# Moving the left-hand block loads of a graph kernel's layer products by one place in the load queue

## The chip, the cores and the metric

The kernel runs on one core of one Trainium2 chip. The metric is the time of the program on the device in microseconds (us), the median of several runs. A profiled execution has a time of its own, and the trace covers its span.

## The reference, cut to what matters

Two graph layers over 3327 nodes (padded to 26 tiles of 128) with 512 features, all in float32:

```python
h = relu(layernorm(x))
q, k, v = h @ Wq.T + bq, h @ Wk.T + bk, h @ Wv.T + bv
x = x + softmax(q @ k.T / sqrt(512) + 2 * adj) @ v      # layer 0
h = relu(layernorm(x))
A2 = adj + eye;  d = diagonal(A2) ** -0.5
x = x + relu((d[:, None] * A2 * d) @ (A2 @ h @ W.T))    # layer 1
```

What costs time are the scores q @ k.T and three large products of a 3328 x 3328 matrix with a 3328 x 512 one: softmax weights times h (g = 0 below), A2 times h (g = 1), A2 times the scaled rows (g = 2).

## The kernel before, in words

**Stages.** First h, its transposes and the projection of the queries; then 52 steps of scores (four groups of 13), which store the weights, with their block sums, in DRAM tensors p; then the layer products. Every product is cut after Strassen's scheme into seven products of half blocks, and each of these once more into seven, so that blocks are added and subtracted by VectorE and multiplied by TensorE.

**The layer products** are 294 steps, built as `Step` (L701): three products g, seven outer products r in the order p5, p1, p6, p7, p2, p3, p4, two strips s of the output, and seven values of t (0 to 5 and None). So number k = ((g * 7 + r) * 2 + s) * 7 + t. A step needs

- a left-hand block `a`, loaded by `Step.load` (L708) through `left` (L680): two DMAs of 448 KB (strip 0) or 384 KB (strip 1), one if t is None. They read p (L688), the sums (L691) or adjT (L695). The blocks lie in a ring of five views (`a_ring`, L673), so that the block of step m takes the view of step m - 5.
- sums of its quarters, by `Step.sums` (L711, three VectorE instructions at L164 to L166), traced two steps ahead.
- a right-hand block, loaded by `Right.load` (L622, DMAs at L620 and L634) five steps ahead and combined by `Right.make` three steps ahead. The loads whose place would be in front of step 0 are in the list `early` (L1213).

`Step.multiply` gives 14 matmul instructions (L732), or 8 where t is None (L723).

**What sets the order.** `run(k)` (L1313) traces one step, and the block `in_order` (L112, L1379) chains the instructions of VectorE, TensorE, GpSimd, ScalarE and SyncE each in the order in which they are traced. Nearly all loads are issued by SyncE (SP); its queue thus follows the text of `run`. Iteration k traces in this order: the left-hand block of step k + 3; the functions that `between[k]` holds and whose names have the word load; the matmuls of step k; `deliver(k)` (L933), which issues stores that were put off; sums of step k + 2; and the remaining functions of `between[k]`. An SP instruction that waits holds up all behind it.

**Other work that SP gets between the steps**: `prepare` (L879, iteration 2: four DMAs of weights, one of a bias, and the diagonal of adjT, `dg`, element by element), `load_diagonal` (L886, iteration 5: the diagonal once more, four DMAs into `by_32`), `Job.load` (iterations 7 to about 161), `other_weights` (L906, iteration 154: four DMAs), `Columns.reload` and `Columns.load` (in g = 2), and the stores of `Columns.add` (L1197), four DMAs in rows of 128 bytes for each of 14 pieces of the output. These are put off by `later` steps and issued by `deliver`. Other stores (`post`, L930) go through ScalarE's queue. `judge` (L834, iteration 8) checks the row sums of the softmax: six small VectorE instructions and then a matmul at L848, which TensorE meets between steps 8 and 9.

The blocks of steps 0 to 2 are loaded during the scores (`openers`), the later ones in `run`:

```python
        if k + 3 < len(steps):
            steps[k + 3].load()
```

Of the kernel before, what the change touches and what calls it, by code (L numbers as in the profile page):

```python
# [47 lines left out]
def graph_layers_kernel(  # L48
# [49 lines left out]
    def bank(k, name):  # L98
        return banks.tile([P, BW], F32, name=name, tag=f"bank{k}")
# [647 lines left out]
    steps = [(n, t) for n in range(len(groups)) for t in range(HALF)]  # L747
# [36 lines left out]
    with in_order(*(e.engine for e in (nc.vector, nc.tensor, nc.gpsimd, nc.sync))):  # L784
# [11 lines left out]
        k = len(steps)  # L796
# [32 lines left out]
    def banks_for(*names):  # L829
        return {r: bank(ROLE[r], r) for r in names}  # L830
# [102 lines left out]
    def deliver(before):  # L933
        while posted and posted[0][0] < before:
            posted.pop(0)[1]()

    def set_up():

        free = [view(k, j)[:, 2 * m : 2 * m + 2] for k, j in ((2, 2), (3, 0), (3, 1), (3, 2)) for m in range(2)]
        free = [f.rearrange("p a w -> p (a w)") for f in free] + [mid(k, [P, H[0]], f"ct{k}") for k in range(10)]  # L940
        for s in range(2):
            cts[s] = [[free.pop()[:, : H[s]] for d in range(DC)] for y in range(2)]
        cts["to"] = [free.pop() for k in range(2)]
# [202 lines left out]
    def turn_last(i):  # L1146
        turned_last[i] = turned(i, LAST[i - 20])
# [54 lines left out]
    steps = [Step(g, r, s, t, rights[g, r, t]) for g in range(3) for r in ORDER for s in range(2) for t in every]  # L1202
# [4 lines left out]
    def number_of(g, r, s, t):  # L1207
        return ((g * len(ORDER) + r) * 2 + s) * len(every) + t

    def at(k, what, *args):  # L1210
        between.setdefault(k, []).append((what, args))

    early = []  # L1213
    for g in range(3):
        for n, r in enumerate(ORDER):
            for t, e in enumerate(every):
                k = number_of(g, n, 0, t)
# [11 lines left out]
    for n, job in enumerate(jobs):  # L1229
        k = k0 + n * (k1 - k0) // len(jobs)  # L1230
# [10 lines left out]
    k = number_of(0, 5, 1, 2)  # L1241
# [6 lines left out]
    k = number_of(1, 5, 1, 2)  # L1248
# [8 lines left out]
    k = number_of(2, 4, 0, 0)  # L1257
# [14 lines left out]
    k = number_of(1, 4, 0, 0)  # L1272
# [2 lines left out]
        at(k + 3 + n, difference)  # L1275
    at(k + 8, turn_sign)

    for what in early:
        for _ in what() or ():
            pass  # L1280
# [4 lines left out]
    def flow(tasks):  # L1285
        for what, args in tasks:
            yield from what(*args) or (None,)

    def first_of(parts):
        while parts:  # L1290
            for _ in parts[0]:
                yield
            parts.pop(0)

    def do(part, n=None):
        for _ in itertools.islice(part, n):
            pass
# [3 lines left out]
    def begin(k, j):  # L1301
        if (k, j) not in begun:
            begun.add((k, j))
            for w, n in inserted.get((k, j), ()):
                w.product(n)

    def coming(k):
        r, s = steps[k].r, steps[k].s
        gathers[r, s] = Gather(r, s, k == len(steps) - len(every))
        coming_banks.update(banks_for("p2", "p3", "p4"))  # L1310
        gathers[r, s].seed(coming_banks, ("p2", "p3", "p4"))

    def run(k):  # L1313
        step, now[0] = steps[k], k
        if k == 0:
            set_up()
            coming(0)
        if k + 3 < len(steps):
            steps[k + 3].load()
        if step.t == 0:  # L1320
            banks_of.update(banks_for("p6", "p7", "p5"), **coming_banks, **banks_for("p1"))
        t = step.t
        for what, args in between.get(k, ()):
            if "load" in what.__name__:
                what(*args)
        gatherer = gathers[step.r, step.s]
        weighs = any((k, j) in inserted for j in range(7))
        if k in sums_of and not waiting:
            do(sums_of.pop(k)())
        for j, _ in enumerate(itertools.chain((None,), step.multiply(banks_of))):  # L1330
            begin(k, j)
            if j == 4 and t == PAIRS - 1 and gatherer.last:
                gatherer.first(banks_of)
            if j == (1 if k and steps[k - 1].t is None else 2) and k in sums_of:

                sums = sums_of.pop(k)()
                do(sums, 4)
                waiting.insert(1, sums)
            elif weighs and j > 0:
                do(first_of(waiting), 2)  # L1340
        deliver(k)
        if t is None:
            if not gatherer.last:
                gatherer.rest(banks_of, ("p2", "p3", "p4"))
                begin(k + 1, 0)
                coming(k + 1)
            do(first_of(waiting))
            if gatherer.last:
                flags.append(nc.values_load(bad, min_val=0, max_val=1))
                for n, names in enumerate((("p2", "p3"), ("p4", "p8"))):  # L1350
                    gatherer.rest(banks_of, names)
                    for i in range(20 + 3 * n, 23 + 3 * n):
                        turn_last(i)
            else:
                gatherer.rest(banks_of, ("p8",))
        added = 2 + (t is None)
        waiting.append(steps[k + 2].sums() if k + 2 < len(steps) else iter(()))
        if t == PAIRS - 1 and not gatherer.last:
            do(first_of(waiting))
            gatherer.first(banks_of)  # L1360
        if t == PAIRS - 1:
            banks_of["p8"] = bank(ROLE["p1"], "p8")
            gatherer.seed(banks_of, ("p8",))
        if t is None and gatherer.r == "p7":
            settle = gatherer.settle()
            resting.extend((itertools.islice(settle, 2), settle))
            added -= 1
        elif t is None:
            waiting.append(gatherer.settle())
        elif resting:  # L1370
            waiting.append(resting.pop(0))
            added += 1
        waiting.append(flow([(what, args) for what, args in between.get(k, ()) if "load" not in what.__name__]))
        if (k + 1, 0) not in inserted and (k + 1, 1) not in inserted:
            do(first_of(waiting))
        while len(waiting) > added:
            do(waiting.pop(0))

    with in_order(*(e.engine for e in (nc.vector, nc.tensor, nc.gpsimd, nc.scalar, nc.sync))):  # L1379
        for k in range(len(steps)):  # L1380
            run(k)
        deliver(len(steps))
        now[0] = len(steps)
        for i in range(20, NT, 2):
            finish(i, nc.scalar)
        deliver(len(steps) + 1)
# [378 lines left out]
```

## Time and profile before

| what | value |
|---|---|
| median of 3 runs | 2150.86 us (2150.09 to 2152.09) |
| the profiled execution | 2151.03 us |
| its span in the trace | 2149.1 us |
| TensorE clock granted | 0.999 of full speed |
| TensorE (PE) matmuls busy | 2136.7 us, 99% |
| VectorE (DVE) busy | 1653.3 us, 77% |
| ScalarE (ACT) busy | 274.0 us, 13% |
| DMA | 592.10 MB, 276 GB/s in the mean |
| SP's queue (q1) | 374056 packets, 532.72 MB |
| left-hand blocks (`part`) | 546 DMAs on SP, 3.8 to 6.0 us from issue to landing (medians by kind) |
| step of 14 matmuls | 5.26 us in strip 0, 4.52 us in strip 1 |

In lines of the profile, PE is a matmul, PEld a weight load, SPq an instruction of SyncE's queue. L164 is line 164 of the kernel. `part<-p` is an instruction that writes a tile of the name part from one named p; `<-DVE most L845` behind a time says what ended the idle time before. The chain of work that ended last is followed back from the end, at each step to what released it.

### The profile page before, as it was taken

What the parts mean: (1) busy time and instruction counts of PE and PEld (TensorE: products, weight loads), DVE (VectorE), ACT (ScalarE), POOL (GpSimd) and SP (SyncE); (2) the same over time, 40 slices, a digit from 0 to 9 for tenths busy, and PEclk for the clock granted to TensorE, in tenths of its full rate; (3) what the DMA queues carried; (4) which work ended last, traced back from release to release, by engine and by line L of the source; (5) the groups of instructions that cost most, each with busy time, mean ns of one, the idle gap of its engine ahead of it and who ended that gap; (6) DMA issues with size and microseconds to landing.
All of it is one profiled execution on the core that took longest, in us unless ns stands there. A gap on an engine that the chain in (4) does not pass through costs nothing.

```text
span 2149.1 us, 20906 instructions
## 1 busy us (share of the span) xinstructions
PE 2136.7 (99%) x6272; PEld 1181.0 (55%) x6272; DVE 1653.3 (77%) x3235; ACT 274.0 (13%) x441; POOL 67.5 (3%) x63
## 2 busy tenths in 40 slices
PE   9999999999999999999999999999999999999998
PEld 5555555555555555555454555555666665555554
DVE  7479888888897688776777778787466666788888
ACT  5312221112110000001111000000111100000000
POOL 2000000000003000000111000000000000000000
PEclk9999999999999999999999999999999999999999
DMA  8678888888999899888787889986656578978897
GB/s 301 216 255 294 298 308 286 307 291 287 345 309 299 292 369 335 284 301 303 263 306 266 301 281 360 326 313 225 194 158 210 155 210 255 303 224 249 267 284 190
DMA packets 402498, 592.10 MB, mean 276 GB/s; under 512 B 139964, under 2 KB 273480, under 8 KB 402376
## 3 DMA queue, kind: packets, MB, share of 16 engines
q1 hardware_dynamic: 374056, 532.72, 75.2%
q10 hardware_dynamic: 28320, 57.95, 7.3%
q8 instruction: 52, 0.85, 0.2%
q14 instruction: 70, 0.57, 0.1%
HBM read 422.71 MB, written 173.87 MB: 278 GB/s over the span
## 4 chain that ended last, share of the span: by engine, by line
PE 94%; DVE 3%; DMA 1%; issue 1%; POOL 0%; SPq 0%; ACT 0%; DVEq 0%
PE p L732 55%; PE Y L542 13%; PE Z L542 6%; PE p L723 5%; PE p L1056 4%; PE pw L1117 4%; PE X L542 3%; PE Y L398 2%; PE Z L398 1%; PE X L398 0%; DMA wk<-in_wk_dram 0%; DVE part L164 0%; DVE st L185 0%; DMA part<-sum 0%; DMA part<-p 0%
## 5 line engine op out<-in xcount | busy, mean ns | idle before, releaser
L732 PE MATMUL p<-part,b 128*128 128x448 f32 (+1 forms) x3528 | 1257.7, 513 | 0.4 <-ACT p L986 0.2
L732 PEld LDWEIGHTS p<-part,b 128*128 128x128 f32 x3528 | 669.7, 190 | 542.0 <-issue 291.7
L164 DVE TENSOR_TENSOR part<-part 128x896 f32<-128x896 f32 (+1 forms) x252 | 256.7, 1019 | 67.5 <-DMA part<-p 24.2
L542 PE MATMUL Y<-qt,hp 128*128 128x448 f32 (+1 forms) x832 | 308.1, 513 | 0.1
L542 PEld LDWEIGHTS Y<-qt,hp 128*128 128x128 f32 x832 | 157.9, 190 | 133.0 <-issue 73.0
L542 PE MATMUL Z<-qt,hp 128*128 128x384 f32 (+1 forms) x416 | 162.2, 512 | 0.0
L166 DVE TENSOR_TENSOR part<-part,part 128x448 f32<-128x448 f32 (+1 forms) x219 | 129.5, 591 | 15.0
L165 DVE TENSOR_TENSOR part<-part,part 128x448 f32<-128x448 f32 (+1 forms) x219 | 129.4, 591 | 7.3
L723 PE MATMUL p<-part,b 128*128 128x448 f32 (+1 forms) x336 | 124.2, 512 | 0.0
L542 PEld LDWEIGHTS Z<-qt,hp 128*128 128x128 f32 x416 | 79.0, 190 | 66.2 <-issue 37.9
L546 DVE SCALAR_TENSOR_TENSOR g<-g,Y 128x384 f32<-128x384 f32 (+1 forms) x156 | 91.5, 586 | 30.0 <-PE Y L542 28.8
L992 ACT COPY part<-p 128x384 f32<-128x384 f32 (+1 forms) x33 | 16.6, 503 | 656.4 <-PE p L732 466.6
L723 PEld LDWEIGHTS p<-part,b 128*128 128x128 f32 x336 | 63.8, 190 | 54.1 <-issue 31.2
L549 ACT ACTIVATE g<-g 128x768 f32<-128x768 f32 (+1 forms) x48 | 43.1, 898 | 345.7 <-DVE g L546 288.0
L542 PE MATMUL X<-qt,hp 128*128 128x384 f32 (+1 forms) x208 | 81.1, 512 | 0.0
L993 DVE TENSOR_TENSOR part<-p,part 128x384 f32<-128x384 f32 (+1 forms) x33 | 19.3, 585 | 66.0 <-PE p L732 58.4
L1056 PE MATMUL p<-w,ct 128*128 128x512 f32 x136 | 61.6, 592 | 0.0
L542 PEld LDWEIGHTS X<-qt,hp 128*128 128x128 f32 x208 | 39.5, 190 | 33.1 <-issue 19.3
L191 POOL TENSOR_TENSOR rstd<-ve,mhalf 128x1 f32<-128x1 f32 x46 | 38.4, 836 | 528.5 <-DVE ve L189 500.6
L1012 DVE TENSOR_TENSOR ct<-p,part 128x448 f32<-128x448 f32 (+1 forms) x72 | 42.3, 609 | 15.9 <-PE p L723 11.8
L1117 PE MATMUL pw<-w,rows 128*128 128x256 f32 x208 | 53.4, 379 | 0.0
L1047 DVE TENSOR_TENSOR job<-job 128x896 f32<-128x896 f32 (+1 forms) x52 | 52.9, 1018 | 0.0
(194 smaller groups left out, 1680.7 us busy)
## 6 DMA issues: line engine op xcount, KB each, us to landing
part<-sum SPq DMA_DIRECT2D x104, 448.0 KB, 5.0
part<-p SPq DMA_DIRECT2D x91, 448.0 KB, 6.0
part<-sum SPq DMA_DIRECT2D x104, 384.0 KB, 4.2
part<-p SPq DMA_DIRECT2D x91, 384.0 KB, 4.8
part<-in_adjT_dram SPq DMA_DIRECT2D x78, 448.0 KB, 5.0
b<-row SPq DMA_DIRECT2D x234, 128.0 KB, 4.8
part<-in_adjT_dram SPq DMA_DIRECT2D x78, 384.0 KB, 3.8
g<-in_adjT_dram SPq DMA_DIRECT2D x52, 448.0 KB, 4.1
```

What stands on the lines that cost most here:

```text
L164: yield nc.vector.tensor_add(o[:, 0:2], g[:, 0:4:3], g[:, 1:2].to_broadcast([P, 2, g.shape[-1]]))
L165: yield nc.vector.tensor_add(o[:, 2], o[:, 1], g[:, 0])
L166: yield nc.vector.tensor_add(o[:, 3], o[:, 2], g[:, 2])
L398: nc.tensor.matmul(ps[:, :w], M[B[name]][:, c, o * P : (o + 1) * P], hp[k][:, A[name], c], start=start and c == 0, stop=c == 1, skip_group ...
L542: nc.tensor.matmul(ps[:, :wd], h_of(self.t, name, k), qt[B[name]][:, k], start=start and k == 0, stop=k == 1, skip_group_check=True)
L546: nc.vector.scalar_tensor_tensor(a[n], a[n], 2.0, ps[:, :wd], op0=ALU.mult, op1=ALU.add if sign > 0 else ALU.subtract)
L549: nc.scalar.activation(g[1], g[1], AF.Exp, **({"bias": pad} if self.t == HALF - 1 else {}))
L723: yield nc.tensor.matmul(ps[("p2", "p3", "p4", "p8")[k]][:, :w], b[:, z], a[:, 0, y], start=k == 3 and not self.seeded, stop=True, skip_gr ...
L732: yield nc.tensor.matmul(ps[r][:, :w], b[:, i], m, start=self.t == 0 and not adds, stop=self.t == PAIRS - 1 and r in ("p1", "p5", "p6", "p ...
L1047: nc.vector.tensor_add(self.a, self.a, self.b)
L1056: nc.tensor.matmul(ps, cts[s][y][d][:, k * P : (k + 1) * P], w[d], start=d == 0, stop=d == DC - 1)
L1117: nc.tensor.matmul(ps, a, W[B[name]][:, c], start=new and c == 0, stop=c == 1, skip_group_check=True)
```

## The change

The block of step 3 is loaded ahead of the list `early`; in `run` the load of a left-hand block comes behind the other loads of the iteration and is that of step k + 4. The ring keeps its five views.

```diff
+    steps[3].load()
     for what in early:
         for _ in what() or ():
             pass
...
         if k == 0:
             set_up()
             coming(0)
-        if k + 3 < len(steps):
-            steps[k + 3].load()
         if step.t == 0:
             banks_of.update(banks_for("p6", "p7", "p5"), **coming_banks, **banks_for("p1"))
         t = step.t
         for what, args in between.get(k, ()):
             if "load" in what.__name__:
                 what(*args)
+        if k + 4 < len(steps):
+            steps[k + 4].load()
         gatherer = gathers[step.r, step.s]
```

## The prediction

> **What bounds the kernel now.** I read the page first: the busy shares and the chain that ended last.
>
> ```profile
> PE 2136.7 (99%) x6272; PEld 1181.0 (55%) x6272; DVE 1653.3 (77%) x3235; ACT 274.0 (13%) x441; POOL 67.5 (3%) x63
> PE 94%; DVE 3%; DMA 1%; issue 1%; POOL 0%; SPq 0%; ACT 0%; DVEq 0%
> ```
>
> TensorE is busy for 2136.7 of 2149.1 us, which leaves 12.4 us. Next I asked where these lie, with the busy time by stretch (columns: the stretch, its length, then busy us and instruction count of PE, PEld, DVE, ACT, POOL, then clock, DMA share, GB/s).
>
> ```profile
> 640.00:660.00 20.00, 19.84 (x57) 10.31 (x56) 11.84 (x23) 1.23 (x5) 1.73 (x1) 1.00 0.91 180
> 660.00:680.00 20.00, 19.41 (x64) 11.23 (x63) 13.27 (x33) 0.63 (x2) 9.00 (x2) 1.00 1.00 374
> 1700.00:2140.00 440.00, 440.00 (x1294) 245.39 (x1293) 342.20 (x624) 28.41 (x57) 0.00 (x0) 1.00 0.83 248
> sum 1540.00, PE 1538.52 PEld 852.77 DVE 1164.99 ACT 126.54 POOL 48.40; mean PE 153.85 PEld 85.28 DVE 116.50 ACT 12.65 POOL 4.84
> ```
>
> The sum runs from 600 to 2140 us, which holds the end of the scores and all layer products: PE idles 1540.00 - 1538.52 = 1.48 us in it. The rest lies in the start and in the last stores, which the change doesn't touch. The largest piece of the 1.48 is in 660 to 680. The PE timeline and the chain there say what it is:
>
> ```profile
> 664.85 0.21 PE L848 MATMUL p<-good,ones 128*1 128x26 f32 x2 [0.59 <-DVE most L845]
> ```
>
> ```profile
> 655.61 6.00 DMA part<-p
> 661.73 0.97 DVE part L164
> 664.70 0.10 DVE most L845
> ```
>
> The matmul of judge (L848), which PE meets between steps 8 and 9, waits 0.59 us for VectorE. VectorE does judge's work behind the sums of step 10, in the order of the program, and these waited for step 10's left-hand block, issued at 655.61 and landed at 661.61. So a late load costs PE time here although step 10 itself is far off. Why it was issued so late, SP's timeline tells:
>
> ```profile
> 627.72 1.00 SPq L688 DMA_DIRECT2D part<-p  x2
> 628.77 2.01 SPq L870 DMA_DIRECT2D w<-in_wvT_dram  x4
> 630.82 1.05 SPq L882 DMA_DIRECT2D bv_sb<-in_bv_dram  x1
> 631.92 0.67 SPq L884 DMA_DIRECT2D dg<-in_adjT_dram  x1
> 632.69 8.71 SPq L688 DMA_DIRECT2D part<-p  x5
> 641.70 10.89 SPq L889 DMA_DIRECT2D by<-in_adjT_dram  x4
> 652.70 3.28 SPq L688 DMA_DIRECT2D part<-p  x4
> ```
>
> By the ring of five, and counting issues, the rows are: the two DMAs of step 5's block; prepare's six; the blocks of steps 6 (one DMA), 7 and 8 (two each); the four of load_diagonal; the blocks of steps 9 and 10. The 8.71 us hold one issue of 6.53 us, step 6's, straight behind dg; a free one takes 0.38.
>
> [...] only 13 KB each, yet the issue behind dg takes 6.53 us and the second of load_diagonal's 6.22, against 0.38 for a 448 KB block. [...] So what stands ahead in SP's queue counts, also for a transfer without a wait. [...] SP's waits for PE are its largest:
>
> ```profile
> SPq L691 <- PE p L732: 224.3, 106, 8.7
> SPq L1197 <- DMA xr<-x1d: 10.3, 1, 10.3
> ```
>
> [...] 84 matmuls take 31.57 us (0.376 each) or 27.09 us (0.3225), stage after stage.
>
> **The change part by part.** Call L(m) the block load of step m, O(i) the other loads of iteration i, D(i) the stores that deliver puts on SP in it, F(i) what else it issues on SP. SP's order is the program's. Before: L(i+3) O(i) D(i) F(i) | L(i+4) O(i+1). After: O(i) L(i+4) D(i) F(i) | O(i+1) L(i+5). Nothing stands between O(i) and L(i+4) but D(i) and F(i), so **where these are empty the queue is the same, instruction for instruction**. Nor does a slot come free sooner: five views, L(m) waits for step m-5 as before. "Four in front" is the place in the text, not the time. No DMA, wait or buffer is added or taken away, and PE, VectorE and ACT get the same work in the same order. What moves, from the code:
>
> (1) L(3), two DMAs, goes ahead of the early right-hand loads (four DMAs of rows). By the count of issues, step 3's block goes out at 594.01 and 604.77 us; its first use is at 622.93 (VectorE's sums). Both sets are issued between 576 and 616, beside full PE. A step earlier or later: 0.
>
> (2) L(6), one DMA, goes ahead of prepare (F(2): four, one and one DMAs, 2.01 + 1.05 + 0.67 us). L(6)'s view was step 1's; the first half of that view is read by PE only in step 1's first two matmuls. PE began step 0's last eight at 622.10, so step 1 at 622.10 + 8 x 0.376 = 625.1; the view is free by some 626, SP arrives at 628.77: no wait. Prepare moves back by one issue, 0.4 to 0.5 us. Then the long issue behind dg falls on L(7). dg lands at 640.29; one block more lies ahead of it, 448 KB at some 378 GB/s (the DMA view's rate at that time) = 1.2 us. The long issue ended 1.07 us ahead of dg's landing (632.69 + 6.53 = 639.22), so now by 640.4; three issues at 0.47 follow: 641.85. load_diagonal began at 641.70, released by the matmul of the totals (L818), with SP free since 641.40. So it starts at about 641.9: **+0.2 us**, and with it L(9), L(10), the sums of step 10, judge, and PE. Bounds: 0 if the long issue keeps its length (632.59 + 0.47 + 0.10 + 6.53 = 639.7, ready by 641.1, hidden by L818's release), and +0.9 if the block's whole 1.2 us comes on top of SP's 641.40.
>
> (3) L(158), two DMAs, goes ahead of other_weights (F(154): four DMAs of 256 KB). They are first needed three iterations on; PE shows no stall from 1360 to 1660. 0.
>
> (4) In the last layer L(261), L(264) and so on to L(291) go ahead of the eleven D of four 128-byte-row stores each. A set costs SP 3.5 to 5.4 us of issue (one 12.49, with the 10.3 us wait above), and lies now behind a block instead of ahead of it. The block comes up to that much earlier; the stores, and the O(i+1) behind them, up to one step (4.5 us) later. Gain for PE: it loses nothing from 1700 to 2140, so 0. Cost: a block is issued near the end of step m-5, four steps of 4.515 us (27.09 / 6) = 18.1 before its use; less 6 us landing and 2.1 for its sums (0.96 + 0.56 + 0.56), **10 us of slack**. The right-hand loads have five steps. A turned buffer comes back after nine steps. 0. If the cover were gone, each us past 10 is a us.
>
> The sum: +0.2, on the profiled execution's 2151.03 (span 2149.1 and 1.93 around it): 2151.2. The median of the runs shown is 0.17 lower: 2151.0.
>
> **The rivals.** *Slower, by the boundary*: load_diagonal starts later than hidden, because prepare is pushed by more than one issue, or dg drains later. From 641.70 on each us of SP is a us of PE, through L(10), VectorE's order and judge. For it: the 0.59 us stall, no slack on this chain. Against: SP has 0.3 us in hand and L(6) needn't wait. Were the whole of step 1 awaited (630.4), prepare would move by 1.7 + 0.5, and the price would be 2.2 - 0.3 = 1.9 us: 2152.8.
>
> *Slower, by a block behind a long wait*: L1197 waits 10.3 us for ACT's load of xr, with which it shares no data[...]. With another order such a wait can fall where a whole row of blocks queues behind it. It decides from 10 us of lateness; say 15, so 5 us: 2156. Against: in the one case seen, blocks behind the 12.49 us set didn't stop PE.
>
> *Faster*: blocks ahead of slow stores and of prepare end VectorE's waits and PE's small gaps. The page bounds it: 1.48 us in all, of which 0.59 at judge: 2149.9. Against: the gaps aren't at the stores.
>
> *It doesn't do what it says* is my forecast's own core: the queue keeps its order.
>
> **How the numbers follow.** Forecast, own range 2150.2 to 2152.0: 0.60. Slower by the boundary, to 2153.2: 0.17. Faster, down to 2149.4: 0.16. Behind a long wait: 0.07. The range 2149.4 to 2153.2 leaves out the last and some tails of the others (runs of one kernel differ by 2 us here). About 0.2% (4.3 us) is what a measurement of this kernel can tell from no change. More than 1.48 us can't be won from the part that changes, so faster gets only 0.02, out of its case's 0.16, for what I can't see; slower 0.08, the long wait's 0.07 and 0.01 of the boundary's; within 0.2%: 0.90.
>
> **What would show it.** In SP's timeline three block issues in a row near 627.7, prepare after them, a long issue on step 7's block, load_diagonal at 641.7 to 641.9; PE's wait at L848 0.5 to 0.9 us; in the last layer the same stores each behind one more pair of blocks; PE idle from 600 to 2140 between 1.2 and 2 us. Wrong would be: new PE waits for VectorE or ACT anywhere in the layers, load_diagonal past 643, or a clearly different order on PE.

## The result, and the profile after

| | before | after |
|---|---|---|
| median | 2150.86 us (2148.88 to 2152.65, 7 runs) | 2158.15 us (2155.94 to 2159.91, 7 runs) |
| profiled execution | 2151.03 us, span 2149.1 | 2159.91 us, span 2157.8 |
| TensorE clock granted | 0.999 | 0.997 |

The ratio of after to before is 1.0034, 95% interval 1.0025 to 1.0044: 7.3 us slower, and outside the predicted range. What happened, as the experiments below show, is the rival to which the prediction gave 0.07, a block behind a long wait.

The page of the kernel after, busy shares and the chain that ended last:

```profile
PE 2140.6 (99%) x6272; PEld 1182.7 (55%) x6272; DVE 1653.8 (77%) x3235; ACT 273.2 (13%) x441; POOL 68.5 (3%) x63
PE 93%; DVE 3%; DMA 2%; issue 1%; ACT 0%; POOL 0%; SPq 0%; ACTq 0%; DVEq 0%
```

Here one sees almost nothing: the shares are those of before, except that 1% of the chain has gone from PE to DMA. The busy time by stretch, with the columns as in the prediction, has it:

```profile
640.00:660.00 20.00, 19.82 (x57) 10.30 (x56) 12.19 (x24) 1.22 (x5) 1.56 (x1) 1.00 0.92 186
660.00:680.00 20.00, 20.00 (x66) 11.62 (x65) 13.09 (x33) 0.70 (x2) 11.62 (x2) 1.00 0.98 354
1700.00:2140.00 440.00, 435.16 (x1272) 242.42 (x1271) 337.22 (x616) 28.01 (x56) 0.00 (x0) 0.99 0.82 246
```

PE now stands still for 440.00 - 435.16 = 4.84 us in the last product, where it lost nothing before. The small hole at 660 to 680 is gone. PE's timeline says that the 4.84 us are one wait, ahead of step 287 (the first of strip 1 of the last outer product):

```profile
2108.91 3.17 PE L723 MATMUL p<-part,b 128*128 128x448 f32 x8
2116.92 13.34 PE L732 MATMUL p<-part,b 128*128 128x384 f32 x34 [4.84 <-DVE part L993]
```

The eight matmuls (L723) are step 286. L993 is VectorE's work on the results of step 285, and the work from there on frees the banks (the pieces of memory that hold the results of matmuls) which step 287 writes. So PE doesn't wait for its own block at all; it waits for an instruction that stands behind that block's sums in VectorE's order. VectorE's timeline of the same kernel:

```profile
2114.11 0.96 DVE L164 TENSOR_TENSOR part<-part 128x768 f32<-128x768 f32 x1 [8.41 <-DMA part<-in_adjT_dram]
2116.24 0.62 DVE L993 TENSOR_TENSOR part<-p,part 128x448 f32<-128x448 f32 x1
```

VectorE stood 8.41 us for the left-hand block of step 287. In the kernel before the same two began at 2104.26 and 2106.39, without a wait. SP's timeline of the kernel after, from where the block should have gone out:

```profile
2088.44 6.94 SPq L1197 DMA_DIRECT2D out_dram<-turned  x4
2096.39 0.36 SPq L695 DMA_DIRECT2D part<-in_adjT_dram  x1
2107.55 0.34 SPq L1181 DMA_DIRECT2D part<-x1c  x1
2107.99 3.63 SPq L695 DMA_DIRECT2D part<-in_adjT_dram  x4
2111.68 4.53 SPq L1197 DMA_DIRECT2D out_dram<-turned  x4
```

and of the kernel before, at the same place:

```profile
2094.11 0.33 SPq L1181 DMA_DIRECT2D part<-x1c  x1
2094.53 1.36 SPq L695 DMA_DIRECT2D part<-in_adjT_dram  x2
2095.94 12.49 SPq L1197 DMA_DIRECT2D out_dram<-turned  x4
2108.53 2.83 SPq L695 DMA_DIRECT2D part<-in_adjT_dram  x4
```

Before, the block of step 287 (the two DMAs at 2094.53) went out and then SP stood still inside a set of stores. After, SP stands still from 2096.75 to 2107.55, ahead of a right-hand load (L1181), and the blocks of steps 287 and 288 are behind it. SP's waits in the kernel after say for what:

```profile
SPq L1181 <- DMA xr<-x1d: 10.7, 1, 10.7
SPq L695 <- DMA xr<-x1d: 2.0, 2, 1.8
```

It is the wait of before, now at other instructions: for the load of `xr`, which ACT issues (`last_load`, L1135) and which has no data in common with a block. ACT can't issue it sooner, because the six `xr` loads stand behind a copy (L992) that waits for a matmul ending at 2104.57; the first goes out at 2105.32 (before: 2104.70).

The whole way is in the chain that ended last (start, length, what):

```profile
2104.60 0.54 ACT part L992
...
2106.30 2.25 DMA xr<-x1d
...
2108.62 5.42 DMA part<-in_adjT_dram
...
2114.11 0.97 DVE part L164
...
2116.24 0.63 DVE part L993
...
2116.92 29.47 PE p L732 x84
```

The way leads from PE to ACT, to ACT's load, over a semaphore (a counter on which an instruction waits; SP went on at 2108.57, 0.02 us after the `xr` load had landed) to SP's block load, to VectorE and back to PE. The last row holds a second loss: the same 84 matmuls took 27.09 us before, 2.38 less. The stretches behind the wait show why (the last three columns are clock, DMA share, GB/s):

```profile
2112.00:2117.00 5.00, 0.16 (x2) 0.09 (x1) 2.65 (x5) 0.00 (x0) 0.00 (x0) 0.74 1.09 312
2117.00:2122.00 5.00, 5.00 (x9) 2.82 (x10) 4.97 (x10) 0.00 (x0) 0.00 (x0) 0.58 1.00 310
2122.00:2127.00 5.00, 5.00 (x17) 2.98 (x16) 4.86 (x8) 0.00 (x0) 0.00 (x0) 1.00 1.11 337
```

The clock fell while PE stood still. Means of 0.74 and 0.58 are those of a clock of 0.5 from 2114.4 to 2121.2, 6.8 us (stretches of 2 us give 0.50 from 2116 to 2120), and PE got through 9 matmuls in 5 us instead of 17. It fell 2.3 us after PE had stopped (2108.91 + 3.17 = 2112.08) and rose 4.3 us after PE had set in again at 2116.92.

From the start of step 286's matmuls to that of the last such group is 2146.22 - 2108.91 = 37.31 us, and was 2138.39 - 2108.28 = 30.11: 7.20 us = 4.84 + 2.38 within rounding. Of the profiled executions' difference the rest is 0.63 us before step 286, the balance of small waits (the largest, 0.84 us near 1318, isn't in every run of the new order: `after_fill5` lacks it), and 0.9 in the end.

### The profile page after: what moved, and what is told of

The parts are those of the page before. It is cut to its first block, busy times and chain, and to the rows that moved or that the text cites. A ratio compares the mean times of both kernels' runs of the same rounds, so it can differ in the third digit from the quotient of the medians.

```text
span 2157.8 us, 20907 instructions
## 1 busy us (share of the span) xinstructions
PE 2140.6 (99%) x6272; PEld 1182.7 (55%) x6272; DVE 1653.8 (77%) x3235; ACT 273.2 (13%) x441; POOL 68.5 (3%) x63
## 4 chain that ended last, share of the span: by engine, by line
PE 93%; DVE 3%; DMA 2%; issue 1%; ACT 0%; POOL 0%; SPq 0%; ACTq 0%; DVEq 0%
PE p L732 54%; PE Y L542 13%; PE Z L542 6%; PE p L723 5%; PE p L1056 4%; PE pw L1117 4%; PE X L542 3%; PE Y L398 2%; PE Z L398 1%; DMA part<-sum 1%; DVE part L164 1%; DMA xt<-in_x_dram 1%; PE X L398 1%; DVE part L165 0%; DMA sum<-job 0%
## 5 line engine op out<-in xcount | busy, mean ns | idle before, releaser
L723 PE MATMUL p<-part,b 128*128 128x448 f32 (+1 forms) x336 | 124.2, 512 | 0.0
L992 ACT COPY part<-p 128x384 f32<-128x384 f32 (+1 forms) x33 | 16.6, 503 | 663.0 <-PE p L732 499.1
L723 PEld LDWEIGHTS p<-part,b 128*128 128x128 f32 x336 | 63.8, 190 | 54.1 <-issue 31.0
L993 DVE TENSOR_TENSOR part<-p,part 128x384 f32<-128x384 f32 (+1 forms) x33 | 19.3, 586 | 62.4 <-PE p L732 59.2
L1012 DVE TENSOR_TENSOR ct<-p,part 128x448 f32<-128x448 f32 (+1 forms) x72 | 42.2, 609 | 15.8 <-PE p L723 11.8
```

What stands on the lines that cost most here:

```text
L723: yield nc.tensor.matmul(ps[("p2", "p3", "p4", "p8")[k]][:, :w], b[:, z], a[:, 0, y], start=k == 3 and not self.seeded, stop=True, skip_gr ...
```

## The experiments

**What ties ACT's load to SP's.** A completion semaphore is here the counter that the built program names for the end of a DMA. In the built program of either kernel the DMAs of SP and ACT take eight of them in turn, in the one order in which the program was built, and of the 1813 DMAs of its main part 1682 (before) or 1683 (after) carry a wait for the one eight places earlier. Why the wait is put there no run shows. How long it lasts the trace shows, 10.7 us at L1181. The text of the kernel chains each engine's own instructions; how ACT's DMAs fall in among SP's it leaves open. Read from the two built programs (places in the turn):

```
before: 1767 SP block 286 | 1768 SP L1181 | 1769, 1771 SP block 287
        1770, 1772, 1773, 1775 to 1777 ACT xr
        1774, 1778 to 1780 SP stores of iteration 284 | 1781, 1782 SP block 288
after:  1766 to 1770, 1772 ACT xr
        1773 SP block 286 | 1774 SP L1181 | 1775, 1776 SP block 287 | 1777, 1778 SP block 288
```

Before, the first SP instruction eight places behind an `xr` load is a store (1778, behind 1770), after it is L1181 (1774, behind 1766) with block 287 next. These are the instructions that wait in the two traces. The programs of the other runs fit as well: each SP line that waits for `xr` in its trace has a DMA eight places behind an `xr` load.

**Theory A**: the loss is this tie. The change moved the `xr` loads a few places forward in the turn, and the hold (the time that SP stands still for them), as long as before, now strikes a block that is needed one step (4.5 us) earlier. **Theory B**: the loss comes from the order that the change intends, blocks ahead of the stores and the next loads behind them. **Theory C**: part of it comes from the early moves, parts (1) to (3) of the prediction. The medians of the kernel before beside the two groups of runs were 2151.20 us (`late_alone`, `early_alone`, `after_xr_sp`, `after_xr283`) and 2150.49 us (the other four). Ratios are to these.

### The late part alone, the early part alone

`late_alone` takes the new order from iteration 249 on, `early_alone` up to 248. The first, against the kernel before:

```diff
-        if k + 3 < len(steps):
+        if k < 250:
             steps[k + 3].load()
...
+        if 249 <= k < len(steps) - 4:
+            steps[k + 4].load()
```

> Only the last part of the change: up to iteration 248 the old order (block of step k + 3 ahead of the other loads), from 249 the new one. Theory A (in the last layer the new order puts ScalarE's six loads of xr, in the turn of the shared completion semaphores, ahead of the block of step 287, which then waits for them): the whole loss, about 7 us, so 2158 us, with SP's load L1181 waiting some 10 us for xr and PE idle 4 to 5 us ahead of step 287. Theory B (the stores of the output pieces now lie between a block and the next loads and hold them up): 2158 us as well. Theory C (the order of the earlier parts, steps 3 to 161): about 2151 us.

> Only the earlier parts of the change: the new order up to iteration 248, the old one from 250. Theories A and B: 2151 us, within 1 us of the kernel before, and the wait for xr at a store (L1197) as there. Theory C: about 2158 us. My forecast for the step at the boundary was +0.2 us at load_diagonal.

`late_alone`: 2157.89 us, ratio 1.0029 (1.0018 to 1.0040). `early_alone`: 2151.15 us, ratio 0.9999 (0.9991 to 1.0008). The loss lies in the last 45 iterations, all of it within the intervals; theory C falls. PE's waits in `late_alone`:

```profile
PE p L732 <- DVE part L993: 4.6, 1, 4.6
```

### The tie taken away

`after_xr_sp` is the kernel after with the `xr` loads on SP, in the order of the text, so that no SP transfer is behind a load that another engine has yet to issue; `before_xr_sp` is the same for the kernel before.

```diff
-            nc.scalar.dma_start(xr[:, k], x1_of(i + k)[:, 0:E])
+            nc.sync.dma_start(xr[:, k], x1_of(i + k)[:, 0:E])
```

> The changed kernel, with the six loads of xr issued on SyncE's queue in place of ScalarE's; the order of blocks and stores stays the new one. Theory A: nothing on SP waits for ScalarE at that place any more, so 2151 us, no idle time of PE ahead of step 287. Theory B: the stores are where they were, so 2158 us.

> The kernel before with the xr loads issued by SyncE instead of ACT, so no SyncE transfer can be held by an ACT load that isn't yet issued. Theory A: SyncE's 10.3 us wait at the store (L1197) shrinks or goes, and since PE didn't stand still there in the kernel before, the time is the same: 2150.5 to 2151.5 us. If the wait at the store cost something hidden, it is faster by 1 us or more.

`after_xr_sp`: 2150.53 us, ratio 0.9997 (0.9989 to 1.0005). The order of blocks and stores is the one of the change, and the loss is gone; theory B had forecast 2158 us. Its stretch from 2100 to 2140:

```profile
2100.00:2140.00 40.00, 40.00 (x121) 22.61 (x120) 35.65 (x58) 1.56 (x3) 0.00 (x0) 1.00 0.78 202
```

`before_xr_sp`: 2150.68 us, ratio 1.0001 (0.9993 to 1.0009). SP no longer waits for `xr`; the hold of 10 us at the stores had cost the kernel before nothing that can be measured. Neither of the two can be told from the kernel before, so there is no better version here.

### The tie without the change

The opposite test: the kernel before, in its own order, with eight tiny loads on SP that nobody reads. They only shift the turns.

```diff
+    spare_rows = const.tile([P, 12], F32, name="spare_rows")
...
+    def load_spare(n):
+        for c in range(n):
+            nc.sync.dma_start(spare_rows[:, c : c + 1], bq[:, 0:1])
+
+    at(283, load_spare, 8)
```

In `before_spare8_283` the first SP transfer eight places behind an `xr` load is block 287; with `at(280, ...)` in `before_spare8_280` it is a store again.

> The kernel before, in its own order of blocks and stores, with eight tiny loads (one column of bq each, never read) put on SyncE at iteration 283. They only shift the turns of the eight completion semaphores: the first SyncE transfer that follows an xr load in its turn is now the block of step 287 and no longer a store. Theory A (the loss is a left-hand block tied to ACT's late xr load): slow without the change, about 2156 to 2158 us, with a PE wait of 3 to 5 us behind VectorE at step 287 or 288. Theory B (the loss comes from where blocks and stores stand in SyncE's queue): as the kernel before, 2151 us, plus at most 1 us for the eight issues.

> The same eight tiny loads three iterations earlier, at 280: the first SyncE transfer tied to an xr load is again a store of iteration 284, as in the kernel before. Theory A: no loss, 2151 to 2152 us, PE without a wait of over 1 us in the last layer. If it is as slow as the kernel with the loads at 283, the eight loads themselves cost the time, and the other run proves nothing.

`before_spare8_283`: 2157.32 us, ratio 1.0035 (1.0021 to 1.0048). `before_spare8_280`: 2150.44 us, ratio 0.9997 (0.9989 to 1.0005). Eight loads of one column make the kernel before as slow as the change does, and the same eight three iterations earlier cost nothing. Theory B falls. SP's waits in the slow one (its lines are one higher, L696 is L695):

```profile
SPq L696 <- DMA xr<-x1d: 9.9, 1, 9.9
```

PE's waits there:

```profile
PE p L733 <- DVE part L994: 3.6, 1, 3.6
```

and SP's in the control, where the hold is again at the stores:

```profile
SPq L1198 <- DMA xr<-x1d: 6.0, 1, 6.0
```

### The tie at another place

`after_xr283` is the kernel after with `last_load` built six iterations sooner, which moves the `xr` loads forward in the turn, the first by 18 places, the last by 3:

```diff
-        at(number_of(2, 6, 1, 2) + n, last_load, i)
+        at(283 + n, last_load, i)
```

> The changed kernel, with the loads of xr traced six iterations earlier (283 to 285 in place of 289 to 291), so that ScalarE issues most of them before its copy at the end of step 285, which waits for PE. They keep their queue and still share the semaphores. Theory A: they land early, nothing is held long, so 2151 us. Theory B: 2158 us.

2153.44 us (2150.98 to 2155.43), ratio 1.0005 (0.9997 to 1.0014): most of the loss is gone, perhaps not all, for the median is 2.24 us above that of the kernel before. That nothing would be held long was wrong: the hold falls in two on other instructions, and blocks still come somewhat late. SP's waits and then PE's timeline:

```profile
SPq L620 <- DMA xr<-x1d: 9.0, 1, 9.0
SPq L1197 <- DMA xr<-x1d: 4.2, 1, 4.2
```

```profile
2111.64 1.64 PE L732 MATMUL p<-part,b 128*128 128x384 f32 x4 [1.51 <-DVE part L993]
2113.55 0.91 PE L732 MATMUL p<-part,b 128*128 128x384 f32 x2 [0.27 <-DVE part L996]
2114.95 10.29 PE L732 MATMUL p<-part,b 128*128 128x384 f32 x31 [0.48 <-DVE ct L1012]
```

PE waits 2.26 us in all, and its clock stays at 1.00. So the length of the hold alone doesn't say its price: 13.2 us of hold cost less here than 10.7 us at L1181.

### The half clock

`after_fill5` puts five matmuls of 512 columns, read by nobody, on PE ahead of step 287, where it stands still.

```diff
+        if k == 287:
+            spot = bank(ROLE["p8"], "filler")
+            for _ in range(5):
+                nc.tensor.matmul(spot, ident, cts[0][0][0][:, 0:BW], start=True, stop=True)
```

> The kernel after, with five matmuls of 512 columns that nobody reads (some 0.86 us each, 4.3 us together) on TensorE ahead of step 287, where PE stood idle for 4.84 us. They add nothing to the wait if they fit in it. If the half clock behind the wait comes from PE's standing still, it goes: 2.1 to 2.4 us less than the kernel after, about 2155.8 us, and no granted clock of 0.5 between 2110 and 2125. If the clock falls for another reason, 2158 us or somewhat more, with the half clock still there.

2156.61 us (2155.63 to 2158.39), ratio 1.0030 (1.0018 to 1.0041). PE's timeline, and the stretches behind:

```profile
2109.19 4.45 PE L1330 MATMUL filler<-ct,ident 128*128 128x512 f32 x10
2114.26 1.64 PE L732 MATMUL p<-part,b 128*128 128x384 f32 x4 [0.62 <-DVE part L993]
2116.17 0.91 PE L732 MATMUL p<-part,b 128*128 128x384 f32 x2 [0.28 <-DVE part L996]
2117.57 12.87 PE L732 MATMUL p<-part,b 128*128 128x384 f32 x39 [0.49 <-DVE ct L1012]
```

```profile
2112.00:2117.00 5.00, 4.11 (x10) 1.27 (x8) 4.72 (x9) 0.00 (x0) 0.00 (x0) 1.00 1.10 233
2117.00:2122.00 5.00, 4.51 (x15) 2.60 (x15) 4.93 (x10) 0.00 (x0) 0.00 (x0) 1.00 1.02 390
```

The clock stays at 1.00, where it was 0.74 and 0.58 in the kernel after, so there it fell because PE stood still. But the gain isn't the 2.38 us: from step 286's matmuls to the last such group are 2142.85 - 2106.18 = 36.67 us, 0.64 less than the 37.31 of the kernel after. A PE at full clock runs up against VectorE, which is as late as in the kernel after: waits of 0.28 us (L996) and 0.49 us (L1012) that the slow PE doesn't meet. They are the half of it; the other half of the 1.5 us by which the 84 matmuls, from start to start, still take longer than before isn't shown as waits. My expectation was wrong in that. In the medians the difference of 1.5 us to the kernel after isn't resolved; the intervals overlap.

## Why the prediction was wrong, point by point

**(1), (3): 0, nothing against it.** `early_alone` holds both parts and (2): ratio 0.9999, interval 0.9991 to 1.0008, some 2 us either way.

**(2): the boundary, right in the order; of its +0.2 us nothing is seen.** SP's timeline of the kernel after:

```profile
628.04 1.63 SPq L688 DMA_DIRECT2D part<-p  x3
629.72 2.20 SPq L870 DMA_DIRECT2D w<-in_wvT_dram  x4
...
634.03 7.54 SPq L688 DMA_DIRECT2D part<-p  x4
641.87 9.12 SPq L889 DMA_DIRECT2D by<-in_adjT_dram  x4
```

There are three block issues in a row, prepare behind them, and the long issue on step 7's block: its first DMA takes 6.11 us, and step 6's, now ahead of dg, 0.39. So it is the place behind dg that makes an issue long, as the prediction said; why, no run shows. load_diagonal starts at 641.87 (predicted 641.7 to 641.9), but not because SP came late. In both kernels it is the matmul of the totals that lets it go:

```profile
SPq L889 <- PE tot L818: 0.2, 1, 0.2
```

SP stands ready 0.2 us earlier both times, and the 0.17 us are PE's, whose matmul is that much later. The shift was hidden, which is the prediction's lower bound, 0. Two waits came here too that weren't there before: dg (0.3 us) and step 7's block (0.7 us) wait for the two DMAs of step 5's block, eight places earlier. They cost nothing.

PE's wait at L848, predicted at 0.5 to 0.9 us, isn't there: load_diagonal's four issues took 9.12 us instead of 10.89. That isn't the change's doing. `late_alone` has the old order here, and took 8.62 us, also without the wait; of all the profiles only the one of the kernel before has the 0.59 us.

**(4): 0, wrong, and the whole loss.** The step that failed is "No DMA, wait or buffer is added or taken away", and with it that SP's order is all that matters. SP's order was what I said. The waits weren't: which DMA an instruction must await depends on how the DMAs of ACT fall in among those of SP, and moving a load by a few lines moved the first `xr` load from between the two DMAs of block 287 to ahead of block 286. In place of "no wait" came one of 10.7 us at L1181, with block 287 behind it, and it cost PE 4.84 us of standing still and 2.38 us of half clock. The sign of being wrong that the prediction named, a new PE wait for VectorE, is what the trace has. Which rule of the builder put it there isn't shown.

The terms of that step, by the trace: the lateness was to be "up to one step (4.5 us)", for the stores and the other loads, while blocks were to come earlier; block 287's first DMA went out at 2107.99 instead of 2094.53, with PE 0.63 us later: 12.83 us late. The slack was to be 10 us: the block had gone out 2111.45 - 2094.53 = 16.92 us ahead of its step's matmuls, not 18.1, and from its issue to PE's start took 2116.92 - 2107.99 = 8.93 us, with L993 (0.62) in it, behind which the banks come free: 7.99 us of slack. The difference of 12.83 and 7.99 is PE's wait of 4.84 us; it must be, for all terms are read from the same two traces, so this shows how large the terms were and proves nothing more. The prediction also gave the sets of stores 3.5 to 5.4 us with one exception; the one at 2112.99 took 7.04 us.

**The rival "behind a long wait" was right in its mechanism, and its price in part by luck**: 15 us late, 10 of slack, 5 us, against 12.83, 7.99 and 4.84. The 15 were a guess, and both terms are some 2 us too large, which cancels. The 2.38 us of half clock behind it are missing. What was wrong above all is its chance, 0.07. I took "blocks behind the 12.49 us set didn't stop PE" as evidence of cover. VectorE's timeline of the kernel before would have told otherwise:

```profile
2114.55 0.29 DVE L713 TENSOR_TENSOR part<-part,ident 128x128 f32<-128x128 f32 x1 [2.43 <-DMA part<-in_adjT_dram]
```

VectorE already stood 2.43 us there for block 288, the block behind the held stores. So the cover was partly used, and the same hold one block earlier has a step (4.5 us) less of it.

**The rivals "slower by the boundary" and "faster"** have nothing left: the boundary cost nothing that the runs show, and no run is faster than the kernel before beyond its interval.

## What to carry to other kernels

When a trace shows a queue waiting for a DMA with which it shares no data, take the tie as part of the schedule. Here edits to the order of DMAs, on either queue, put it on other instructions: 10.3 us at L1197 in the kernel before, 10.7 us at L1181 with the change, 9.9 us at a block with eight loads more on SP, 9.0 us at L620 with ACT's loads built sooner. Price it by who stands behind each neighbour and how much cover these have, and give it a chance to match. Here a load that can be issued only late went better on the queue of those it was tied to in the changed kernel (2150.53 us), and no worse in the kernel before (2150.68 us). And count, behind a PE wait of several us, what a slower clock adds: here the 84 matmuls behind waits of 3.61, 4.61 and 4.84 us took 2.87, 2.73 and 2.38 us longer.

## What the runs showed of the hardware that wasn't expected

PE waits of 3.61 us (`before_spare8_283`), 4.61 us (`late_alone`) and 4.84 us (the kernel after) were followed by matmuls at half clock; three short waits of 1.51 us at most (`after_xr283`) weren't. What lies between wasn't tried.

The slow stretch was as long behind each of the three waits. Worked out from the mean clock of stretches of 2 us, it began 2.1, 2.8 and 2.3 us after PE had stopped and lasted 6.8 us in each trace. So a shorter wait left more of it to the matmuls: the 84 matmuls behind it took 29.96, 29.82 and 29.47 us, and 27.09 in the kernel before. A PE wait of 3.61 us thus came with 2.87 us of slow matmuls, one of 4.84 us with 2.38.

Filling the wait with idle matmuls kept the clock up and yet won only 0.64 us in the trace. The waits there that the trace shows say that VectorE was next in line.
